# A convolution-attention layer with a sorted mixture of experts on one core: row outputs on another engine, shares and counts a step later, first halves apart, two pairs in both directions

## The chip, the cores and the metric

The kernel runs on one core of a Trainium2 chip. The metric is the device time in microseconds (us) of one execution. Of the engines, TensorE (PE) multiplies matrices, VectorE (DVE), ScalarE (ACT) and GpSimd (POOL) work on elements, and SyncE (SP) issues most of the transfers between the core's memory and DRAM. Each engine takes its own list of instructions, and semaphores hold them back until what they need is there.

## The reference

The input x has 4 batches of 32 channels, 128 x 128, all float32. Each batch becomes a matrix q of 128 rows (32 channels times 2 x 2 pixel places) by 4096 columns. Note the axis: the rows of the similarity matrix are q's *columns* as the kernel lays them out, 4096 of them in groups of 128.

```python
xs = x.reshape(B, C, h, R, w, R).transpose(0, 1, 3, 5, 2, 4).reshape(B, C * R * R, h, w)
energy = jnp.einsum('bci,bcj->bij', q, q)              # (4096, 4096), symmetric
d = jnp.sqrt(jnp.diagonal(energy, axis1=1, axis2=2))
attn = jax.nn.softmax(energy / (d[:, :, None] * d[:, None, :]), axis=-1)
out = gamma * jnp.einsum('bcj,bij->bci', q, attn).reshape(...) + xs
...
t = t + _L1_attn_ref(_ln_t(t), Wk, Wq, Wv)             # linear attention, 8 heads
t = t + _L1_ffn_ref(_ln_t(t), router_w, router_b, expert_w, expert_b)   # 2 of 8 experts for each token
```

The first layer is a softmax attention without separate queries and keys, so the matrix before the division by the row sums is symmetric. The second layer treats the result as 4096 tokens of 128 numbers per batch: layer norm, a linear attention over the whole batch, layer norm, a router, and for each token a weighted sum of two expert products.

## The kernel before

**Attention.** The 4096 columns of a batch are eight chunks of 512. `attend` walks rows i = 0 to 7, and in row i the chunks jc = i (the diagonal) and 0 to i - 1. One step is one group of 128 rows of chunk jc against the 512 columns of chunk i: a product `pe` (L497), its exponential `pr` with the sums over columns (L500, ScalarE), and two steps later the product `po` (L404) that adds to the row's output. Since the matrix is symmetric, a pair (i, jc) is exponentiated once. What chunk jc gets from it needs the transposed block: VectorE transposes 32 x 32 blocks of pr into F (L356), `move` writes F to DRAM as `blocks`, `bring` reads it back as G in another order (L455), and `transposed_share` multiplies it (`pg`, L362), takes its sums on ScalarE (`junk`, L367) and adds the result to the earlier chunk's output `o` (L372, VectorE). A share is four sub-steps, at most one for each step, and each needs the one PSUM bank `pg`; the row output needs the one bank `po`. When a row's last product is done the bank is copied out as `o` (L409), and only then can the next row's first `po` begin.

For the last row of the last batch, pairs with jc of 4 or more do not go by DRAM: G is made by 16 direct transfers. The very last pair (7, 6) has no F at all; it is computed in both directions, that is, with four more products `pe_back`, four more exponentials and four products `back` (L462 on).

**Time in the program.** TensorE, VectorE, ScalarE and SyncE run in the program's own order (`manual_schedule`), so the order in which the Python code issues is the order in each queue; GpSimd has its own. The code keeps a `clock` in units of a 128 x 128 product: a step adds 8, a share's sub-step 4, so a full step has 12. A share is due when the clock has passed `LAG` since its G was asked for. Other work is cut into generators, and each `yield` ends a piece:

```python
timed.append((setup_sorting(), 58, 70, 9))     # (pieces, begin %, end %, count) of a batch's attention
...
if clock[0] >= stream[1]:
    stream[1] = clock[0] + PACE                # PACE = 10: a piece of layer 1 about every step
```

Every call of a stream advances it by two yields. From 84% of a batch's attention on, its `layer1` joins the stream and runs under the next batch's attention; only the last batch's has nothing to run under and ends in `last_parts`.

**prep** loads a quarter of a batch (two chunks, L275, four transfers on SP's queue), transposes it (`ptq`, L306; `qT`, L295), takes squares and sums (L317, L318), the power -1/2 on GpSimd (L166, `rn`), scales (`qs`, L327) and transposes back (`ptn`, L335) into the two normalised chunks `qn` (L333). For the first quarter of the first batch all of it stands ahead of the first step.

**layer1.** `close_rows(kc)` finishes a quarter, once both of its chunks have all their shares: sums and reciprocals (`den`, `rd`, `rdx`, L613 to L618), their transposes (`pbd`, L640), the division (`df`, L627), the residual (L647), statistics (L650, L563 to L571), normalised rows (L577, on VectorE L660) and the Gram matrix (`pgram`, L602), with the transposes `ptx` (L582) of the last batch. In batches 0 to 2 the tokens are sorted by expert: `sorted_experts` adds up one-hot rows (`runs`, L843 to L846, VectorE), counts them by a product (`pcnt`, L853), works out places (to L887), scatters rows to DRAM `xs` with GpSimd's indirect transfers (L902), loads tiles of one expert, multiplies (`pys`, L958), stores `ys`, and gathers them (L1020) into the sum (L992). `setup_sorting` makes constants and fills xs eight times 624 KB from x on ScalarE's queue (L156), so that unused rows hold numbers.

Of the kernel before, what the change touches and what calls it, by code (L numbers as in the profile page):

```python
# [12 lines left out]
F32 = mybir.dt.float32  # L13
BF16 = mybir.dt.bfloat16
U32 = mybir.dt.uint32
AF = mybir.ActivationFunctionType
ALU = mybir.AluOpType
# [5 lines left out]
def kernel(  # L23
# [44 lines left out]
    nc = tc.nc  # L68
    P = 128
    B, C, H, W = x.shape  # L70
    N = (H // 2) * (W // 2)
    NB = N // P
    CH = 512
    NCH = N // CH
    NJ = CH // P
# [12 lines left out]
    ppool = ctx.enter_context(tc.tile_pool(name="ppool", bufs=6))  # L88
# [11 lines left out]
    def psum_t(name):  # L100
        return ps_t.tile([P, CH], F32, tag="pt", name=name)
# [63 lines left out]
    def pow_neg_half(dst, src):  # L165
        pinned(nc.gpsimd.tensor_tensor(dst, src, neg_half.to_broadcast(list(src.shape)), ALU.pow))  # L166
# [100 lines left out]
    def tokens(ap, b):  # L267
        return ap[b].rearrange("c (s k r) w -> s r c k w", s=2, r=2)

    def load_tokens(dst, b, k0, nk):  # L270
        src = tokens(x, b)
        for s in range(2):
            for r1 in range(2):
                p0 = s * 64 + r1 * 32
                nc.sync.dma_start(dst[p0 : p0 + 32], src[s, r1, :, k0 : k0 + nk, :])  # L275


    def prep(b, kc, st):

        if b == 0:  # L280
            if kc == 0:
                st["all"] = big1.tile([P, 4, 8, HW2, 2], F32, tag="T", name="xx_0")
            xx = st["all"][:, kc]
        else:
            xx = xin.tile([P, 8, HW2, 2], F32, tag="xx", name=f"xx_{b}_{kc}")
        load_tokens(xx.rearrange("p k w r -> p k (w r)"), b, 8 * kc, 8)
        qT = qpool.tile([P, 2, NJ, P], F32, tag="qT", name=f"qT_{b}_{kc}")
        st.setdefault("qT", {})[2 * kc] = qT[:, 0]
        st["qT"][2 * kc + 1] = qT[:, 1]
        yield  # L290
        yield
        yield from idle(1)

        def load_half(g, pt):
            nc.vector.tensor_copy(  # L295
                qT[:, :, 2 * g : 2 * g + 2, :].rearrange("p s j (r c) -> p (j r) s c", c=64),
                pt.rearrange("p (m s c) -> p m s c", s=2, c=64),
            )

        for g in range(2):  # L300
            yield
            pt, done = hold(f"ptq_{b}_{kc}_{g}", partial(load_half, g))
            for jj in range(2):
                for r2 in range(2):
                    k = 4 * g + 2 * jj
                    nc.tensor.transpose(  # L306
                        pt[:, ts(2 * jj + r2, P)], xx[:, k : k + 2, :, r2].rearrange("p k w -> p (k w)"), ident
                    )
            yield
            done()  # L310
        yield
        yield
        ss = stat.tile([P, 2 * NJ], F32, tag="ss", name=f"ss_{b}_{kc}")
        rn = stat.tile([P, 2 * NJ, 1], F32, tag="rn", name=f"rn_{b}_{kc}")
        for s in range(2):
            sq = work.tile([P, NJ, P], F32, tag="qs", name=f"sq_{b}_{kc}_{s}", bufs=2)
            nc.vector.tensor_tensor(sq, qT[:, s], qT[:, s], ALU.mult)  # L317
            nc.vector.tensor_reduce(ss[:, ts(s, NJ)], sq, AX.X, ALU.add)  # L318
            if s == 1:
                pow_neg_half(rn[:, :, 0], ss)  # L320
            yield
            yield
        yield from idle(1)
        scaled = []
        for s in range(2):
            qs = work.tile([P, NJ, P], F32, tag="qs", name=f"qs_{b}_{kc}_{s}", bufs=2)
            nc.vector.tensor_tensor(qs, qT[:, s], rn[:, ts(s, NJ)].to_broadcast([P, NJ, P]), ALU.mult)  # L327
            scaled.append(qs)
        for s, qs in enumerate(scaled):
            yield  # L330
            qn = npool.tile([P, CH], F32, tag="qn", name=f"qn_{b}_{2 * kc + s}")
            st.setdefault("qn", {})[2 * kc + s] = qn
            pt, done = hold(f"ptn_{b}_{kc}_{s}", lambda p, qn=qn: nc.scalar.activation(qn, p, AF.Copy))  # L333
            for j in range(NJ):
                nc.tensor.transpose(pt[:, ts(j, P)], qs[:, j, :], ident)  # L335
            yield
            done()
        yield
        yield
# [2 lines left out]
    tick = [0]  # L342
    queued = []
    late = []
    LAG = 45
    exps = []

    def after(ticks, f):
        queued.append((tick[0] + ticks, f))
# [32 lines left out]
    def attend(b, st):  # L382
# [11 lines left out]
        for i in range(NCH):  # L394
            ending = b == B - 1 and i == NCH - 1
            order = list(range(i - 1)) + [i, i - 1] if ending else [i] + list(range(i))
            row = {"left": NJ * (i + 1) + NJ - 1}

            def values(w, blk, lo, hi, i=i, row=row):
                start = "po" not in row  # L400
                if start:
                    row["po"] = ps_o.tile([P, CH], F32, tag="po", name=f"po_{b}_{i}")
                row["left"] -= 1
                nc.tensor.matmul(  # L404
                    row["po"][:, lo:hi], qT[blk // NJ][:, blk % NJ, :], w, start=start, stop=(row["left"] == 0)
                )
                if row["left"] == 0:
                    o = opool.tile([P, CH], F32, tag="o", name=f"o_{b}_{i}")
                    nc.vector.tensor_copy(o, row["po"])  # L409
                    st["o"].append(o)  # L410

            def below(tiles, blks, i=i, values=values):
# [19 lines left out]
                done()  # L432

            def move(F, i, jc):
                last = b == B - 1 and i == NCH - 1 and jc >= NCH - 4
                if last:
                    G = gpool.tile([P, 4, NJ, P], F32, tag="G", name=f"G_{b}_{i}_{jc}")
                    for a in range(4):
                        for q in range(4):
                            nc.sync.dma_start(  # L440
                                G[ts(q, S), a].rearrange("p ib f -> p (ib f)"),
                                F[ts(a, S), q].rearrange("p ib j c -> p (ib j c)"),
                            )
                    late.append((clock[0] + 58, transposed_share(b, st, i, jc, G)))
                    return
                blocks = dram.tile([4, S, 4, CH], F32, tag="blocks", name=f"blocks_{b}_{i}_{jc}", bufs=4)
                nc.sync.dma_start(
                    blocks.rearrange("a p q f -> (a p) q f"), F.rearrange("p q ib j c -> p q (ib j c)")
                )
                after(3, partial(bring, blocks, i, jc))  # L450
# [6 lines left out]
                    )  # L457
                late.append((clock[0] + LAG, transposed_share(b, st, i, jc, G)))

            def back(w, j, i=i):  # L460

                if j == 0:  # L462
                    while len(held) > 1:
                        held[0]()
                    banks[0] = 2
                    row["back"] = psum_t(f"back_{b}")
                nc.tensor.matmul(row["back"], qT[i][:, j, :], w, start=(j == 0), stop=(j == NJ - 1))
                if j == NJ - 1:
                    nc.vector.tensor_tensor(st["o"][i - 1], st["o"][i - 1], row["back"], ALU.add)
                    st["got"][i - 1] += 1  # L470
                    banks[0] = 3

            for jc in order:
                both = ending and jc == i - 1
                for j in range(NJ if both else 0):
                    yield
                    tick[0] += 1
                    pe = ps_e.tile([P, CH], F32, tag="pe", name=f"pe_{b}_back_{j}")
                    nc.tensor.matmul(pe, qn[i][:, ts(j, P)], qn[jc], start=True, stop=True)
                    pr = ppool.tile([P, CH], F32, tag="pr", name=f"pr_{b}_back_{j}")  # L480
                    nc.scalar.activation(pr, pe, AF.Exp, accum_out=sums[:, NJ * i + j, jc : jc + 1])
                    after(2, partial(back, pr, j))
                    turn_tick()
                    clock[0] += 2 * NJ
                    step_share()
                    yield
# [48 lines left out]
    def layer1(b, st):  # L535
# [290 lines left out]
        def sorted_experts(h):  # L826
# [18 lines left out]
            while shift < HR:  # L845
                nc.vector.tensor_tensor(dst[:, pad:], src[:, pad:], src[:, pad - shift : pad - shift + HR], ALU.add)  # L846
                src, dst = dst, src
                shift *= 2
            yield
            run = src[:, pad:]  # L850
            counts, places = small("count", [P, 2, E]), small("at", [P, HR, 1])
            pc, done = hold(f"pcnt_{b}_{h}", lambda p: nc.vector.tensor_copy(counts.rearrange("p n e -> p (n e)"), p[:, : 2 * E]))
# [343 lines left out]
    first = prep(0, 0, states[0])  # L1196
    next(first)
    load_weights()
    for _ in first:
        pass  # L1200

    ordered = ExitStack()
    ordered.enter_context(tc.manual_schedule(engines=ENGINES))
    timed = []
    for b in range(B):

        if b == 0:
            for kc, begin, end in ((1, 0, 5), (2, 6, 20), (3, 25, 45)):
                timed.append((prep(0, kc, states[0]), begin, end, 12))
            timed.append((setup_weights(), 46, 58, 9))  # L1210
            timed.append((setup_sorting(), 58, 70, 9))
        if b + 1 < B:
            nxt = states[b + 1]
            timed.append((prep(b + 1, 0, nxt), 66, 82, 12))
# [72 lines left out]
```

## Time and profile before

| | us |
|---|---|
| median of 3 runs | 1778.02 |
| lowest and highest | 1777.36, 1779.36 |
| profiled execution | 1780.28 |
| its span, first to last instruction | 1778.5 |
| TensorE busy | 1672.9 (94%) |
| VectorE, ScalarE busy | 899.4, 912.0 (51% each) |
| GpSimd busy | 514.6 (29%) |
| DMA, mean over the span | 187 GB/s |

In the profile PE is TensorE's matmuls and PEld its weight loads. A float32 product is two instructions and so stands as x2. Time in brackets is what the engine sat idle just before, with the instruction that ended the wait. Busy time of TensorE runs past its real end, since matmuls are pipelined: the distance between starts is the true price. Times within a run count from the first instruction.

### The profile page before, as it was taken

What the parts mean: (1) busy time and instruction counts of PE and PEld (TensorE: products, weight loads), DVE (VectorE), ACT (ScalarE), POOL (GpSimd) and SP (SyncE); (2) the same over time, 40 slices, a digit from 0 to 9 for tenths busy, and PEclk for the clock granted to TensorE, in tenths of its full rate; (3) what the DMA queues carried; (4) which work ended last, traced back from release to release, by engine and by line L of the source; (5) the groups of instructions that cost most, each with busy time, mean ns of one, the idle gap of its engine ahead of it and who ended that gap; (6) DMA issues with size and microseconds to landing.
All of it is one profiled execution on the core that took longest, in us unless ns stands there. A gap on an engine that the chain in (4) does not pass through costs nothing.

```text
span 1778.5 us, 20656 instructions
## 1 busy us (share of the span) xinstructions
PE 1672.9 (94%) x5572; PEld 890.8 (50%) x5572; DVE 899.4 (51%) x2249; ACT 912.0 (51%) x2843; POOL 514.6 (29%) x553
## 2 busy tenths in 40 slices
PE   7999999999999999989999999999999999889787
PEld 4544544455554555445554455545555455434533
DVE  3333333456475335565468334556647533455587
ACT  3455444464565544445565554546456554445366
POOL 1000000011017604550014631661101760670156
PEclk9999999999999999999999999999999999999799
DMA  2666788854557989884357789996445699995001
GB/s 59 166 178 166 214 235 249 222 130 121 152 150 220 265 235 266 240 263 120 122 163 215 231 242 260 262 255 187 136 151 149 214 271 250 269 281 132 1 13 36
DMA packets 218563, 332.91 MB, mean 187 GB/s; under 512 B 24528, under 2 KB 136656, under 8 KB 204368
## 3 DMA queue, kind: packets, MB, share of 16 engines
q1 hardware_dynamic: 202192, 299.18, 60.2%
q0 software_dynamic: 12288, 25.19, 4.8%
q10 hardware_dynamic: 3968, 7.22, 1.3%
q8 instruction: 46, 0.75, 0.2%
q14 instruction: 69, 0.57, 0.1%
HBM read 172.50 MB, written 162.00 MB: 188 GB/s over the span
## 4 chain that ended last, share of the span: by engine, by line
PE 66%; DMA 15%; DVE 13%; issue 2%; SPq 2%; ACT 2%; POOL 1%; DVEq 0%; ACTq 0%; POOLq 0%
PE po L404 20%; PE pe L497 17%; PE pg L362 15%; DMA ys<-xn 4%; DMA blocks<-F 4%; PE py L1099 2%; DMA G<-blocks 2%; DVE F L356 2%; PE pgram L602 2%; PE pys L958 2%; DMA yb<-ys,place 2%; PE pat L714 1%; DMA xx<-in_x_dram 1%; DVE df L627 1%; PE ptd L430 1%
## 5 line engine op out<-in xcount | busy, mean ns | idle before, releaser
L500 ACT ACTIVATE pr<-pe 128x512 f32<-128x512 f32 (+1 forms) x576 | 322.9, 561 | 592.4 <-PE pe L497 572.9
L404 PE MATMUL po<-pr,qT 128*128 128x512 f32 (+3 forms) x1152 | 555.3, 564 | 13.4 <-DVE o L409 13.0
L362 PE MATMUL pg<-G,qT 128*128 128x512 f32 x888 | 457.9, 597 | 28.3 <-DVE o L372 21.8
L497 PE MATMUL pe<-qn,qn 128*128 128x512 f32 x896 | 460.7, 596 | 0.7 <-ACT pr L500 0.6
L356 DVE STREAM_TRANSPOSE F<-pr 128x512 f32<-128x512 f32 x444 | 311.5, 704 | 199.8 <-ACT pr L500 198.5
L404 PEld LDWEIGHTS po<-pr,qT 128*128 128x128 f32 x1152 | 216.6, 192 | 258.8 <-issue 230.2
L367 ACT ACTIVATE junk<-G 128x512 bf16<-128x512 f32 x444 | 275.4, 620 | 6.8 <-issue 4.6
L362 PEld LDWEIGHTS pg<-G,qT 128*128 128x128 f32 x888 | 163.4, 191 | 216.1 <-issue 157.4
L1020 POOL DMA_INDIRECT yb<-ys,place x192 | 186.5, 971 | 265.9 <-ACT pr L500 138.5
L902 POOL DMA_INDIRECT xs<-xn,place x192 | 186.1, 969 | 110.8 <-ACT pr L500 53.0
L497 PEld LDWEIGHTS pe<-qn,qn 128*128 128x128 f32 x896 | 155.7, 192 | 118.9 <-issue 111.8
L372 DVE TENSOR_TENSOR o<-o,pg 128x512 f32<-128x512 f32 x111 | 75.4, 679 | 212.0 <-PE pg L362 211.8
L940 DVE COPY xn<-pys 128x256 f32<-128x256 f32 (+1 forms) x120 | 49.2, 416 | 216.4 <-DMA ys<-xn 120.0
L166 POOL TENSOR_TENSOR rn<-ss,neg_half 128x8 f32<-128x8 f32 x16 | 29.5, 1841 | 377.1 <-DVE ss L318 377.0
L500 ACT ACTIVATION_READ_ACCUMULATOR pr<-pe 128x1 f32 x576 | 111.9, 194 | 0.0
L935 ACT ACTIVATE xn<-pys 128x256 f32<-128x256 f32 (+1 forms) x120 | 44.9, 378 | 122.5 <-PE pys L965 122.5
L166 POOL TENSOR_TENSOR rsf<-dm_f,neg_half 128x8 f32<-128x8 f32 (+1 forms) x15 | 26.2, 1744 | 259.1 <-DVE sv_f L569 259.1
L958 PEld LDWEIGHTS pys<-ew_sb,xn 128*128 128x128 f32 x468 | 69.0, 191 | 56.6 <-issue 44.6
L992 DVE SCALAR_TENSOR_TENSOR acc<-yb,weight,acc 128x128 f32<-128x128 f32 x192 | 64.1, 339 | 62.7 <-DMA yb<-ys,place 42.8
L497 PE MATMUL pe<-qn 128*128 128x512 f32 (+3 forms) x256 | 92.2, 444 | 0.0
L166 POOL TENSOR_TENSOR rsa<-dm_a,neg_half 128x8 f32<-128x8 f32 x16 | 26.3, 1641 | 217.3 <-DVE sv_a L569 217.3
L367 ACT ACTIVATION_READ_ACCUMULATOR junk<-G 128x1 f32 x444 | 85.0, 191 | 0.0
(178 smaller groups left out, 1549.0 us busy)
## 6 DMA issues: line engine op xcount, KB each, us to landing
blocks<-F SPq DMA_DIRECT2D x109, 1024.0 KB
G<-blocks SPq DMA_DIRECT2D x436, 256.0 KB
xn<-xs SPq DMA_DIRECT2D x114, 128.0 KB
ys<-xn SPq DMA_DIRECT2D x114, 128.0 KB
xx<-in_x_dram SPq DMA_DIRECT2D x64, 128.0 KB
T<-in_x_dram SPq DMA_DIRECT2D x64, 128.0 KB
out_dram<-acc SPq DMA_DIRECT2D x128, 64.0 KB
t<-T SPq DMA_DIRECT2D x12, 512.0 KB
```

Source lines behind the costliest of these rows:

```text
L166: pinned(nc.gpsimd.tensor_tensor(dst, src, neg_half.to_broadcast(list(src.shape)), ALU.pow))
L356: f()
L362: nc.tensor.matmul(pg.rearrange("p (a f) -> p a f", a=4), st["qT"][i][:, ib, :], G[:, :, ib], start=(ib == 0), stop=(ib == NJ - 1),)
L367: nc.scalar.activation(junk, G[:, :, ib], AF.Copy, accum_out=st["sums"][:, NJ * i + ib, jc : jc + 1])
L372: nc.vector.tensor_tensor(o, o, pg.rearrange("p (a j c) -> p a j c", a=4, c=S), ALU.add)
L404: nc.tensor.matmul(row["po"][:, lo:hi], qT[blk // NJ][:, blk % NJ, :], w, start=start, stop=(row["left"] == 0))
L497: nc.tensor.matmul(pe[:, c0:], qn[jc][:, ts(j, P)], qn[i][:, c0:], start=True, stop=True)
L500: nc.scalar.activation(pr[:, c0:], pe[:, c0:], AF.Exp, accum_out=sums[:, t, i : i + 1]).ins
L902: inst = nc.gpsimd.indirect_dma_start(xs[h], offset(place[:, i, k : k + 1]), xn[:, k, :], None)
L958: nc.tensor.matmul(p[:, 2 * P + j * D : 2 * P + j * D + D], bufs[4 + g % 2][:, j, :], weights[:, bass.ds(begins[2 * (g % 2) + j], D)], sta ...
L992: nc.vector.scalar_tensor_tensor(a[:, k % 4, :], yb[k // 4][:, i, k % 4, :], weight[:, i, k, :], a[:, k % 4, :], ALU.mult, ALU.add)
L1020: inst = nc.gpsimd.indirect_dma_start(yb[k // 4][:, i, k % 4, :], None, ys, offset(place[:, i, k : k + 1]))
```

## The change

Row outputs are copied out of PSUM by ScalarE. `LAG` is 57 instead of 45. `sorted_experts` has two more yields between the runs and the count. The first quarter's loads are split over two queues, its powers are taken for each half by itself, and what is left of it after the first chunk's `qn` joins the timed work of the first batch. The last row of the last batch takes both of its last pairs, (7, 5) and (7, 6), in both directions, and the direct transfers serve pairs 3 and 4. `setup_sorting` is spread up to 98% of the first batch.

```diff
-    def load_tokens(dst, b, k0, nk):
+    def load_tokens(dst, b, k0, nk, queues=(nc.sync, nc.sync)):
...
-                nc.sync.dma_start(dst[p0 : p0 + 32], src[s, r1, :, k0 : k0 + nk, :])
+                queues[r1].dma_start(dst[p0 : p0 + 32], src[s, r1, :, k0 : k0 + nk, :])
...
-        load_tokens(xx.rearrange("p k w r -> p k (w r)"), b, 8 * kc, 8)
+        first = b == 0 and kc == 0
+        load_tokens(
+            xx.rearrange("p k w r -> p k (w r)"), b, 8 * kc, 8, (nc.sync, nc.scalar if first else nc.sync)
+        )
...
-            if s == 1:
+            if first:
+                pow_neg_half(rn[:, ts(s, NJ), 0], ss[:, ts(s, NJ)])
+            elif s == 1:
                 pow_neg_half(rn[:, :, 0], ss)
...
-    LAG = 45
+    LAG = 57
...
+            twice = (i - 2, i - 1) if ending else ()
...
-                    nc.vector.tensor_copy(o, row["po"])
+                    nc.scalar.activation(o, row["po"], AF.Copy)
...
-                last = b == B - 1 and i == NCH - 1 and jc >= NCH - 4
+                last = b == B - 1 and i == NCH - 1 and jc >= NCH - 5
...
-            def back(w, j, i=i):
+            def back(w, j, jc, i=i):
...
-                    nc.vector.tensor_tensor(st["o"][i - 1], st["o"][i - 1], row["back"], ALU.add)
-                    st["got"][i - 1] += 1
+                    nc.vector.tensor_tensor(st["o"][jc], st["o"][jc], row["back"], ALU.add)
+                    st["got"][jc] += 1
...
-                both = ending and jc == i - 1
+                both = jc in twice
...
-                    after(2, partial(back, pr, j))
+                    after(2, partial(back, pr, j, jc))
...
                 shift *= 2
+            yield
+            yield
             yield
             run = src[:, pad:]
...
-    for _ in first:
-        pass
+    while 0 not in states[0].get("qn", {}):
+        next(first)
+    next(first)
...
-    timed = []
+    timed = [(first, 0, 1, 4)]
...
-            timed.append((setup_sorting(), 58, 70, 9))
+            timed.append((setup_sorting(), 58, 98, 9))
```

More of the change, by code (lines that the diff above doesn't have):

```diff
@@ L465, in back @@
                     banks[0] = 2
-                    row["back"] = psum_t(f"back_{b}")
+                    row["back"] = psum_t(f"back_{b}_{jc}")
                 nc.tensor.matmul(row["back"], qT[i][:, j, :], w, start=(j == 0), stop=(j == NJ - 1))
                 if j == NJ - 1:
-                    nc.vector.tensor_tensor(st["o"][i - 1], st["o"][i - 1], row["back"], ALU.add)
-                    st["got"][i - 1] += 1
+                    nc.vector.tensor_tensor(st["o"][jc], st["o"][jc], row["back"], ALU.add)
+                    st["got"][jc] += 1
                     banks[0] = 3
             for jc in order:
-                both = ending and jc == i - 1
+                both = jc in twice
                 for j in range(NJ if both else 0):
@@ L477, in attend @@
                     tick[0] += 1
-                    pe = ps_e.tile([P, CH], F32, tag="pe", name=f"pe_{b}_back_{j}")
+                    pe = ps_e.tile([P, CH], F32, tag="pe", name=f"pe_{b}_back_{jc}_{j}")
                     nc.tensor.matmul(pe, qn[i][:, ts(j, P)], qn[jc], start=True, stop=True)
-                    pr = ppool.tile([P, CH], F32, tag="pr", name=f"pr_{b}_back_{j}")
+                    pr = ppool.tile([P, CH], F32, tag="pr", name=f"pr_{b}_back_{jc}_{j}")
                     nc.scalar.activation(pr, pe, AF.Exp, accum_out=sums[:, NJ * i + j, jc : jc + 1])
-                    after(2, partial(back, pr, j))
+                    after(2, partial(back, pr, j, jc))
                     turn_tick()
```

## The prediction

> **What bounds the kernel now.** I read the page first, then the table of waits, then the timelines of TensorE, VectorE and ScalarE at the longest waits, and last the chain that ended last. The page's own rows say that TensorE sets the time: it is busy 94% of the span, and its slices are nines but for a few places.
>
> ```profile
> PE   7999999999999999989999999999999999889787
> ...
> L404 PE MATMUL po<-pr,qT 128*128 128x512 f32 (+3 forms) x1152 | 555.3, 564 | 13.4 <-DVE o L409 13.0
> ```
>
> A product of 512 columns stands as x2 and 1.02 us, but the next starts 0.86 us after it; so 0.43 us is the price of one of the two, and 128 columns cost 0.11. Taking these prices from every start-to-start distance leaves 145.8 us of the span in which TensorE did not advance at full speed. Only that can be won. Who ends these pauses:
>
> ```profile
> PE pg L362 <- DVE o L372: 21.8, 15, 3.6
> PE po L404 <- DVE o L409: 13.0, 9, 3.6
> ...
> PE pcnt L853 <- DVE runs L846: 6.2, 3, 2.1
> ```
>
> Columns are total us, times, longest. The last two are touched by the change. Their longest cases in TensorE's timeline:
>
> ```profile
> 410.61 0.59 PE L497 MATMUL pe<-qn 128*128 128x256 f32 x2
> 414.79 2.08 PE L404 MATMUL po<-pr,qT 128*128 128x512 f32 x2 [3.58 <-DVE o L409]
> ...
> 519.39 1.02 PE L362 MATMUL pg<-G,qT 128*128 128x512 f32 x2
> 522.48 0.39 PE L853 MATMUL pcnt<-runs,rank_below 128*128 128x8 f32 x2 [2.06 <-DVE runs L846]
> ```
>
> and what VectorE and then ScalarE did at the first of them:
>
> ```profile
> 413.52 0.61 DVE L618 TENSOR_SCALAR rdx<-rd,gam 128x256 f32<-128x256 f32 x2
> 414.05 0.68 DVE L409 COPY o<-po 128x512 f32<-128x512 f32 x1
> ```
>
> ```profile
> 417.33 0.28 ACT L500 ACTIVATE pr<-pe 128x128 f32<-128x128 f32 x1 [5.61 <-PE pe L497]
> ```
>
> The row's sum was complete at about 410.8, yet VectorE copied it at 414.05, behind a whole closing block (den, rdx and the statistics before them). ScalarE meanwhile had nothing from 411.7 to 417.3. In the last two rows of TensorE the count is asked for while VectorE still adds up the runs.
>
> The third place is a transfer that comes late, in the table by stretch and in the chain of waits:
>
> ```profile
> 240.00:290.00 50.00, 43.99 (x104) 19.30 (x103) 16.31 (x24) 19.85 (x60) 0.00 (x0) 0.97 0.91 269
> ```
>
> ```profile
> 245.84 5.48 DMA xs<-in_x_dram
> 251.38 6.10 DMA blocks<-F
> ...
> 259.17 4.51 DMA G<-blocks
> 263.68 3.48 issue
> ```
>
> The last three numbers of the stretch are clock, DMA share and GB/s: the eight fills of xs, 624 KB each, have the DMA engines 91% busy, and a block on its way to DRAM and back waits behind them. The fourth place is the end of attention, in the chain:
>
> ```profile
> 1662.40 0.62 DVE rdx L618 x2
> ...
> 1675.09 2.08 PE pgram L602 x8
> ```
>
> In the same chain the last product takes 0.86 from 1655.28, to 1656.14; the last quarter's rdx is made only at 1662.4, since VectorE first closes the quarter before.
>
> **What the Trainium skill says.** "PSUM — Partial Sum Buffer", section "Engine vs sequencer instructions": ScalarE and VectorE take their queues strictly in order. The trace agrees: the copy at 414.05 stood behind rdx for 3.3 us with its input ready. "TensorE: Matmul & The Clock Gate", part 1, on the clock gate: after idling the array runs at half rate until a free-running window of activity has passed. The trace agrees: the product after the 414.79 stall has 2.08 us in place of 1.02. So a stall costs more than its idle time. "DMA: Bandwidth & Descriptors", "Issuing engines are not separate DMA queues": a second issuer saves only issue time. The trace of before cannot tell; it has one issuer at the start.
>
> **The change part by part.** The sum is made against the profiled execution, 1780.3 us (span 1778.5), which is 2.3 above the median; the same 2.3 is taken off at the end.
>
> *Row outputs on ScalarE.* 32 copies leave VectorE (0.69 each) and 32 of 0.60 come to ScalarE, the duration of its qn copy of the same form; the skill's price for such a copy (page "VectorE: DVE Perf Modes", the errata section) gives an estimate of 0.66 against 0.57, the same order. Only the place in the queue matters. Loss by the pitch, over the 9 to 10 us around each of the three long stalls (414.8, 837.1, 1257.5): 5.5, 5.4, 5.4, half-rate products included. Nine more waits, at 27, 42, 67, 549, 705, 971, 1126, 1392 and 1456, have 0.4 to 1.0 each, 5.3 together. On ScalarE the copy is behind one exponential and ahead of the next, and done some 0.9 us after the sum. The long stalls go; what is late next is rdx: without the stall pbd would be asked for near 413.5, and VectorE has rdx at 414. I leave 0.9 each for that: 16.3 - 2.7 = 13.6. Of the small ones, the rows that have no share to stand between keep theirs: 5.3 - 1.5 = 3.8. Behind the copy on ScalarE stand the share's sum over G (0.62 + 0.19) and the next exponential; products two steps later wait for that one, and a step has 2.58 us of TensorE against some 2.1 of ScalarE with the copy, so nothing. Sum 17.4 (bounds 12 and 20).
>
> *Shares a step later.* LAG + 12 is one step. No instruction and no DMA is added; a share's four products and its o add (L372) move by a step. G has 2.6 us more to arrive, its buffer is free 2.6 later, with four steps to spare before the third block after it is brought. It puts a share of 0.86 between a row's last product and the next row's first, which is part of what I counted above; alone 0 (bounds -5 and +3, since an o add may fall before or behind a closing block).
>
> *Counts a step later.* The three stalls cost 4.5, 2.8 and 4.5 with their half-rate products: 11.7. VectorE has the runs at 522.4; TensorE would ask at 519.39 + 0.86 + 2.58 = 522.8. They go by 0.4 us, so I take 10.5 (bounds 6 and 11.7). Everything behind moves too: 32 scatters of 0.97 on GpSimd per half, the loads and stores on SP's queue, the gathers, by a step per half, 5 us at a batch's end. The last batch that sorts ends its gathers at 1602 and the kernel ends at 1778: hidden. The next batch's closing needs its sort done, which is so at 1554, and begins at 1611.
>
> *Fills of xs over 58 to 98% instead of 58 to 70.* Eight issues on ScalarE's queue, 0.50 each, now some 18 us apart instead of 5. TensorE lost 8.5 us between 262 and 285. From 285 to 405 the DMA share is 0.83 and then 0.46, so there is room. 7 (bounds 3 and 8.5).
>
> *First rows' halves.* Two of four loads go to ScalarE's queue, ahead of its three small ones and the table load; its first work comes at 15.7, so these are hidden. An issue takes 0.60 (eight in 4.79), so the last is issued 1.2 earlier, and SP's next four too; the bytes cannot come faster, I take 0.8. The power is split: one more GpSimd instruction of 1.67, which delays the second half only. The first half no longer waits for the second's reduction (0.6): 0.8 + 0.6 = 1.4. Against it, four transposes and one copy enter the first row, where TensorE waits for ScalarE anyway: 0. I take 1.4 (bounds 0 and 2.2).
>
> *Last two pairs in both directions.* For pair 5 of the last row go four transposes of VectorE (0.70), four shares (0.86 on TensorE, 0.81 on ScalarE) and one G; in come four pe and four back products (0.86 each) and four exponentials. Net +3.4 on TensorE; VectorE gains 2.8; SP has 5 DMAs fewer, since pair 3 takes over the 16 direct ones. Gain: chunks 4 and 5 are complete nine steps before the end, by the order of steps, instead of two. Their closing (pbd 0.4, two gram groups 1.8) and the quarter before's two transposes (0.9) go under attention, where TensorE has no gap: 3.4 + 3.1 = 6.5 later. Then the end: from the last product to the copied gram 23.6 us (1656.14 to 1679.77). After: 1.0 for the copy, 2.8 df, 1.2 T, 1.7 statistics, 1.0 their close, 1.9 GpSimd, 0.6 to the first gram, 3.8 for gram without the transposes between: 14.0. Gain 9.6 - 6.5 = 3 (bounds -1 and 6).
>
> *Not shown by any row:* what VectorE, no longer stalled with TensorE, makes late next. Loss of 2 taken (bounds -3 and 8, the largest being a wait of half a us in two steps of each batch's closings).
>
> Sum: 17.4 + 10.5 + 7 + 1.4 + 3 - 2 = 37.3. 1780.3 - 37.3 - 2.3 = 1740.7.
>
> **The rivals.** *The DMA-bound stages take it back.* From 640 to 800, 1060 to 1230 and 1430 to 1625 the DMA engines are 93 to 94% busy, and TensorE loses 46 us there, mostly at pg behind an o add that waits behind a gathered row. Sorting a step later and shares a step later set these anew. For it: a time set by transfers does not shrink with TensorE's. Against: the transfers are the same. A third more, 15 us: 1756. *The waits only change their names* (the change does not do what it says): the long row stalls become waits for rdx and pg, the runs are still not ready. Then 13.6 and 10.5 are missing: 1765. Against: ScalarE's empty stretch above. *Slower:* the copy is in ScalarE's queue before the row's last product has ended and holds the next exponential, so that TensorE runs out of pr. It decides from 0.62 us a row (the other gains, 19.9, over 32 rows); at 1.0 a row the time is 1778 + 32 - 19.9 = 1790. Against: at 410.8 the next product's exponential could start only at 411.2 anyway.
>
> **How the numbers follow.** Forecast 0.75, alone 1731 to 1751; the DMA stages 0.13; names only 0.07; slower 0.05. The range 1730 to 1760 takes in the first two. About 0.2%, 3.6 us, is what a measurement of this kernel can tell from no change: faster 0.93, same 0.02, slower 0.05.
>
> **What would show it.** po waits on o for under 3 us in all, none over 1; no wait of pcnt over 0.3; no pause of 3 us between 245 and 405; the first pe near 15; the last quarter's rdx within 2 us of the last product. Wrong if ScalarE's exponentials at row starts lie later than TensorE can bear, if the loss in the three DMA stages grows by over 10 us, or if rdx or pg takes over stalls of 3 us at 413, 836 and 1256.

## The result, and the profile after

The changed kernel takes 1750.95 us, median of 4 runs (1748.38 to 1754.33), against 1778.28 us for the kernel before in the same comparison: a ratio of 0.9847, interval [0.9825, 0.9869]. That is 27.3 us less; the forecast, 1740.7, would have been 37.6 less. The profiled execution took 1748.38 us, its span is 1746.6.

The page of the changed kernel, TensorE's slices and the row of the products that the rows' sums are made of:

```profile
PE   7999999999999999989999999999999999989777
...
L410 PE MATMUL po<-pr,qT 128*128 128x512 f32 (+3 forms) x1152 | 550.4, 560 | 0.5 <-ACT o L415 0.5
```

The slices hardly differ (near the end one 8 has become a 9 and, in the tail, another a 7): tenths of 44 us are too coarse for this change. But the idle time in front of these products fell from 13.4 us to 0.5. The table of waits of the changed kernel (total us, times, longest):

```profile
DVE acc L1000 <- DMA yb<-ys,place: 40.1, 31, 3.8
PE pg L367 <- DVE o L377: 25.3, 13, 6.2
DVE acc L1000 <- DMA acc<-t: 22.1, 4, 6.3
...
PE pys L966 <- DVE xn L948: 8.3, 3, 4.0
...
PE pbd L646 <- DVE rdx L624: 1.8, 1, 1.8
...
PE po L410 <- ACT o L415: 0.5, 2, 0.3
```

The row of po is the smallest of those shown, and TensorE has no row any more in which pcnt waits for the runs. But pg, which the change was not aimed at, waits longer than before (its longest rose from 3.6 us to 6.2), and VectorE's wait for the load of acc has risen to 22.1 us; in the kernel before it was 10.2:

```profile
DVE acc L992 <- DMA acc<-t: 10.2, 3, 4.6
```

So something was gained and something was given back. To see how much of each and where, I took TensorE's loss in the prediction's way (start-to-start distances, less 0.43 us per 512 columns) and cut it by stage. "Sort" reaches from a batch's first scatter to 5 us after its last gather is issued, "counts" is the 20 us before each first scatter, "rows" is all else up to the last product (from 25 to 200 us, from 200 us to the first counts, the first rows of batches 1 and 2, and what is left of attention). Every number is of the profiled execution, in us:

| kernel | to 25 us | rows | counts | sort, batches 0, 1, 2 | last product to gram | after it | sum |
|---|---|---|---|---|---|---|---|
| before | 9.4 | 40.6 | 13.0 | 15.3, 15.3, 13.8 | 18.2 | 20.2 | 145.8 |
| changed | 8.8 | 10.2 | 5.1 | 22.3, 17.9, 17.4 | 10.7 | 19.1 | 111.5 |
| difference | -0.6 | -30.4 | -7.9 | +13.2 | -7.5 | -1.1 | -34.3 |

TensorE's own work is 1622.0 us in place of 1618.6, 3.4 more for the second pair, as forecast; -34.3 + 3.4 = -30.9, and the two spans differ by 31.9; the first product also starts 0.94 earlier (5.80 in place of 6.74), which this sum does not count. **The aimed-at stalls went; the stages that sort and gather took 13 us back.**

How it looks where the gain is. In the stretch from 240 to 290 us of the changed kernel, the table by stretch (same columns as before):

```profile
240.00:290.00 50.00, 50.00 (x134) 23.74 (x133) 18.29 (x27) 25.74 (x84) 1.63 (x1) 1.00 0.84 234
```

TensorE is busy for all of 50 us (43.99 before) and the DMA share is 0.84 in place of 0.91. At the first row of the next batch, where TensorE stood for 3.58 us, ScalarE's timeline and then TensorE's:

```profile
399.21 0.60 ACT L415 ACTIVATE o<-po 128x512 f32<-128x512 f32 x1 [0.28 <-PE po L410]
```

```profile
400.30 1.02 PE L410 MATMUL po<-pr,qT 128*128 128x512 f32 x2
...
405.71 0.60 PE L646 MATMUL pbd<-ident,rdx 128*128 128x128 f32 x4
```

The copy follows the row's sum at once; the next row's first product at 400.30 and pbd at 405.71 have no bracket, so neither waits: the wait for rdx that I feared in its place did not come.

How it looks where the loss is: TensorE of the changed kernel at the first closing of batch 1, while batch 0 gathers.

```profile
764.97 1.02 PE L410 MATMUL po<-pr,qT 128*128 128x512 f32 x2
772.23 2.08 PE L367 MATMUL pg<-G,qT 128*128 128x512 f32 x2 [6.24 <-DVE o L377]
774.10 1.92 PE L503 MATMUL pe<-qn,qn 128*128 128x512 f32 x2
775.80 1.91 PE L410 MATMUL po<-pr,qT 128*128 128x512 f32 x2
777.51 1.42 PE L367 MATMUL pg<-G,qT 128*128 128x512 f32 x2
```

VectorE and SyncE's queue in the same place:

```profile
764.00 0.74 DVE L1000 SCALAR_TENSOR_TENSOR acc<-yb,weight,acc 128x128 f32<-128x128 f32 x2 [5.97 <-DMA acc<-t]
764.65 2.78 DVE L633 TENSOR_TENSOR df<-o,pbd 64x512 f32<-64x512 f32 x4
...
768.72 1.22 DVE L653 TENSOR_TENSOR T<-T,df 128x1024 f32<-128x1024 f32 x1
769.97 0.87 DVE L656 BATCH_NORM_STATS2 bs_a<-T 128x6 f32<-128x128 f32 x4
...
771.49 0.69 DVE L377 TENSOR_TENSOR o<-o,pg 128x512 f32<-128x512 f32 x1
```

```profile
753.08 1.75 SPq L461 DMA_DIRECT2D G<-blocks  x4
754.92 1.86 SPq L1010 DMA_DIRECT2D out_dram<-acc  x4
756.99 0.34 SPq L1026 DMA_DIRECT2D acc<-t  x1
```

Read it backwards. TensorE waits for the o add (L377, 771.49). That add stands behind a whole closing block (df, T, statistics) in VectorE's queue, and the block stands behind one gathered row's sum that waits 5.97 us for acc, which was asked for at 756.99, right behind four stores, which in turn stand behind a read of G. What "PSUM — Partial Sum Buffer", section "Engine vs sequencer instructions", says in the Trainium skill, that VectorE takes its queue strictly in order, is what makes a 6 us wait for one row of a sum into a 6 us wait of TensorE: nothing of the closing block needed acc. After it the products take up to 2.08 us in place of 1.02, and start up to 1.87 us apart in place of 0.86; this agrees with what "TensorE: Matmul & The Clock Gate", part 1, on the clock gate, says of an array that has idled.

### The profile page after: what moved, and what is told of

The parts are those of the page before. It is cut to its first block, busy times and chain, and to the rows that moved or that the text cites. A ratio compares the mean times of both kernels' runs of the same rounds, so it can differ in the third digit from the quotient of the medians.

```text
span 1746.6 us, 20682 instructions
## 1 busy us (share of the span) xinstructions
PE 1666.0 (95%) x5580; PEld 891.6 (51%) x5580; DVE 878.6 (50%) x2213; ACT 929.6 (53%) x2875; POOL 509.2 (29%) x554
## 5 line engine op out<-in xcount | busy, mean ns | idle before, releaser
L503 PE MATMUL pe<-qn,qn 128*128 128x512 f32 x896 | 463.9, 600 | 1.8 <-ACT pr L506 1.8
L503 PEld LDWEIGHTS pe<-qn,qn 128*128 128x128 f32 x896 | 155.7, 192 | 117.4 <-issue 107.9
L377 DVE TENSOR_TENSOR o<-o,pg 128x512 f32<-128x512 f32 x110 | 75.1, 682 | 235.0 <-PE pg L367 234.7
L166 POOL TENSOR_TENSOR rn<-ss,neg_half 128x8 f32<-128x8 f32 (+1 forms) x17 | 26.8, 1578 | 459.7 <-DVE ss L321 401.4
L503 PE MATMUL pe<-qn 128*128 128x512 f32 (+3 forms) x256 | 91.4, 439 | 0.7 <-ACT qn L338 0.7
```

The costliest lines, as they stand in the source:

```text
L377: nc.vector.tensor_tensor(o, o, pg.rearrange("p (a j c) -> p a j c", a=4, c=S), ALU.add)
L503: nc.tensor.matmul(pe[:, c0:], qn[jc][:, ts(j, P)], qn[i][:, c0:], start=True, stop=True)
```

## The experiments

Three comparisons of four kernels. The first ran on another chip, on which the kernel before takes 1833.5 us and the changed kernel was not run, so those four are set against each other and against the kernel before; the second and the third, each on a chip of its own, have the changed kernel among them. Times are medians, losses are of the one profiled execution of each kernel. The kernel before was profiled only beside the first result. The sort stages of the changed kernel lost 57.6, 65.5 and 60.7 us in its three profiles, so a difference of a few us between two kernels tells nothing there.

### Four parts undone, one at a time

**u_rows**, the copies on VectorE again:

```diff
-                    nc.scalar.activation(o, row["po"], AF.Copy)
+                    nc.vector.tensor_copy(o, row["po"])
```

> The changed kernel (1751 us) with the row outputs copied by VectorE again, all else kept. Theory A (the parts add, by the places where they act): the waits of po on o come back, long ones at the first row of batches 1 to 3, softened or not by the share that now stands there; 13 to 20 us slower, 1764 to 1771. Rival B (the later share alone had filled those pauses): within 4 us of the changed kernel, and at most 3 us of waits of po on o.

**u_lag**, the shares at their old time:

```diff
-    LAG = 57
+    LAG = 45
```

> The changed kernel with LAG at 45 again, all else kept. Theory A (the later share only covers the short row pauses, since ScalarE took the long ones): 2 to 5 us slower, 1753 to 1756, the loss in the three transfer-bound stages unchanged near 51 us. Rival B (the later share is what gave back 5 to 7 us in those stages): 3 to 7 us faster, 1744 to 1748, and that loss back near 46.

**u_counts**, the counts at their old time:

```diff
                 shift *= 2
-            yield
-            yield
             yield
```

> The changed kernel without the two added yields ahead of the count. Theory A (the later count saves its three stalls, partly given back in a wait of pg on an o add some 1.5 us long in each batch): 6 to 8 us slower, 1757 to 1759, stalls of pcnt of 2 us back and those of pg at the second count gone. Rival B (the step later is also what set the long pauses in the transfer-bound stages, 6.2 and 4.5 us at pg and 4.0 at pys): these vanish too, and the time is within 2 us of the changed kernel.

**u_xs**, the fills of xs close together again:

```diff
-            timed.append((setup_sorting(), 58, 98, 9))
+            timed.append((setup_sorting(), 58, 70, 9))
```

> The changed kernel with the eight fills of xs pressed into 58 to 70% again. Theory A (G and the next quarter come late behind the fills): 6 to 9 us slower, 1757 to 1760, with 6 to 9 us of TensorE's loss between 240 and 290. Rival B (a share that is due a step later waits 2.6 us longer for G, so the later share had removed the worst of it already): 2 to 5 us slower, 1753 to 1756, and no single pause over 2 us at pg there.

Measured, with TensorE's loss in three of the stages and the part of "rows" from 200 us to the first counts, us:

| kernel | time | ratio to before | rows | of it 200 to counts | counts | sort |
|---|---|---|---|---|---|---|
| u_rows | 1812.99 | 0.9879 [0.985, 0.9909] | 17.3 | 6.7 | 5.1 | 114.6 |
| u_lag | 1800.53 | 0.9819 [0.9795, 0.9844] | 16.0 | 6.8 | 5.7 | 100.0 |
| u_counts | 1788.51 | 0.9752 [0.9723, 0.9781] | 10.2 | 4.4 | 7.2 | 91.7 |
| u_xs | 1812.0 | 0.9859 [0.9826, 0.9892] | 18.0 | 12.1 | 5.1 | 110.1 |

The stages outside the sort can be read. Putting the fills back brings 12.1 - 4.4 = 7.7 us of loss, in the two places where it was before; TensorE's timeline of u_xs:

```profile
267.51 1.10 PE L367 MATMUL pg<-G,qT 128*128 128x512 f32 x2 [3.49 <-DMA G<-blocks]
275.73 0.99 PE L309 MATMUL ptq<-ident,xx 128*128 128x128 f32 x4 [1.98 <-DMA xx<-in_x_dram]
```

So the fills are worth what was forecast (7), and the later shares don't cover for them. Putting the copies back costs only 17.3 - 10.2 = 7.1 us at the rows, far less than the 17.4 of the forecast. And the version without the later counts is the fastest of the four: its counts stay cheap (7.2, not 13.0), since LAG 57 alone takes most of those stalls.

Of what was expected, theory A of u_xs holds where it acts (7.7 us, with a pause of 3.49 at pg). u_rows lies between its two theories: 7.1 us at the rows, where po waits for its copy 7.9 us in all but never over 2.2. In u_counts the 2 us waits of pcnt did not come back (none is over 0.7). The times that were expected beside the changed kernel can't be compared on this chip. The sort stages of this chip lose twice what they lose elsewhere; that is told of in the last section, and no verdict is built on it.

### The gain alone, and the two small parts

**after_again** is the changed kernel once more.

> The changed kernel itself, as the measure for the others of this group, since the first group ran where the kernel before takes 1833 us. Theory C (there the whole machine answers later by the same share): ratio to before 0.985 as at first. Rival D (the later signals of that place fall on the transfer-bound stages, which the later steps made tighter): 0.977 to 0.982 or, if they hit the changed kernel harder, over 0.988; without the added yields the ratio was 0.975 there.

**rows_xs** is the kernel before with two edits of the change alone:

```diff
-                    nc.vector.tensor_copy(o, row["po"])
+                    nc.scalar.activation(o, row["po"], AF.Copy)
...
-            timed.append((setup_sorting(), 58, 70, 9))
+            timed.append((setup_sorting(), 58, 98, 9))
```

> The kernel before with two parts alone: row outputs copied by ScalarE, fills of xs spread to 98%. Theory A (parts add by place: 20 us of row pauses and 8.5 us beside the fills): 27 us faster than before where that takes 1778, ratio 0.984 to 0.987, so these two alone bring what the whole change brings. Rival E (without the later share the row pauses only shrink, and the freed time is lost again in the transfer-bound stages): 10 to 18 us faster, ratio 0.990 to 0.994.

**u_pairs**, only the last pair in both directions:

```diff
-            twice = (i - 2, i - 1) if ending else ()
+            twice = (i - 1,) if ending else ()
...
-                last = b == B - 1 and i == NCH - 1 and jc >= NCH - 5
+                last = b == B - 1 and i == NCH - 1 and jc >= NCH - 4
```

> The changed kernel with only its very last pair in both directions, and the direct transfers for pairs 4 and 5, as before. Theory A (9.6 us less at the end against 6.5 us more work under attention): 2 to 4 us slower than the changed kernel of this group, with the last quarter's rdx some 6 us after the last product again. Rival F (the end is bound by the last quarter's own chain and the work moved costs as much as it saves): within 1.5 us.

**u_first**, the first rows prepared at one go from one queue:

```diff
-        first = b == 0 and kc == 0
+        first = False
...
-    while 0 not in states[0].get("qn", {}):
-        next(first)
-    next(first)
+    for _ in first:
+        pass
...
-    timed = [(first, 0, 1, 4)]
+    timed = []
```

> The changed kernel with the first quarter prepared in one piece and loaded by SyncE alone, as before. Theory A: 1.4 to 1.8 us slower than the changed kernel of this group, the first pe at 16.3 in place of 14.2. Rival G (the half that is left comes into the first row at half clock and takes back what the earlier start gives): the first row's output is copied within 0.5 us of the same moment, and the time is the same.

Measured, the kernel before at 1784.37 here:

| kernel | time | ratio to before | rows | counts | sort | last product to gram |
|---|---|---|---|---|---|---|
| after_again | 1754.38 | 0.9833 [0.9817, 0.9849] | 10.3 | 5.1 | 65.5 | 11.1 |
| rows_xs | 1760.63 | 0.9876 [0.9855, 0.9897] | 20.0 | 12.2 | 44.3 | 17.3 |
| u_pairs | 1759.81 | 0.9857 [0.9835, 0.9879] | 12.0 | 5.1 | 62.8 | 17.0 |
| u_first | 1751.89 | 0.9823 [0.9807, 0.9839] | 10.2 | 5.1 | 59.7 | 11.1 |

Two edits of six bring 23.7 of the 30.0 us, and they leave the sort stages where they were in the kernel before (44.3 against 44.4, the latter from the profile beside the first result). So neither the copies nor the fills are what raised the loss there. The remaining edits take 9.7 more at the rows, 7.1 at the counts and 6.2 at the end, and are worth only 6.3 us together, because the sort stages lose more. The 21 us by which the two profiles differ there are too many, though: the profiled execution of after_again is the slowest of its five (1759.19) and that of rows_xs the fastest of its five (1755.87). If all of that scatter lies in the sort stages, some 12 are left at the medians (an estimate from these distances: 4.8 and 4.8).

rows_xs brings a little less than its theory A had (27 us, ratio up to 0.987).

Without the second pair the time is 5.4 us more, where theory A had 2 to 4 (the intervals overlap a little); by the stages the end loses 17.0 - 11.1 = 5.9 more, less the 3.4 of work saved. TensorE's timeline of u_pairs has the place:

```profile
1640.16 0.60 PE L588 MATMUL ptx<-ident,xn 128*128 128x128 f32 x4
1653.76 6.07 PE L608 MATMUL pgram<-xn 128*128 128x128 f32 x32 [12.99 <-ACT xn L583]
```

With it, in the changed kernel, the same stretch is split and shorter:

```profile
1635.90 0.60 PE L646 MATMUL pbd<-ident,rdx 128*128 128x128 f32 x4
1645.74 3.45 PE L608 MATMUL pgram<-xn 128*128 128x128 f32 x16 [8.28 <-ACT xn L583]
1649.57 2.10 PE L703 MATMUL pgv<-wvx,gram 128*128 128x408 f32 x6 [0.38 <-DVE gram L687]
```

The first rows' halves show no gain: u_first is 2.5 us below its control, with intervals that overlap, and its loss up to 25 us is 9.5 against 9.7. Its first pe starts at 15.57 instead of 13.96, but the first row's output is copied at 25.95 against 25.75, and in the other two profiles of the changed kernel at 25.09 and 26.58. That is rival G.

### The two later steps, together, alone and neither

What is left are the two edits that set work a step later. The four corners of that square: **after_third** (both, the changed kernel), **u_counts_again** (shares later, the edit of u_counts), **u_lag_again** (counts later, the edit of u_lag) and **no_steps** (both of these edits, so neither is later).

> The changed kernel itself, the measure for the three others, which leave out the later count, the later share, and both. Theory H (steps that were moved later make the transfer-bound sort stages lose more): ratio 0.983 to 0.986, and TensorE's loss over the three sort stages 55 to 66 us, where the kernel before and the kernel with two parts alone had 44.

> The changed kernel without the two yields ahead of the count. Theory H: the sort stages lose 42 to 50 us instead of 55 to 66, the stretch around each count 2.4 instead of 1.7, and the time is 8 to 15 us under the changed kernel of this group. Rival A (parts add: the later count saves its stalls): 2 to 8 us over it.

> The changed kernel with LAG at 45. Theory H: the sort stages lose 5 to 10 us less, the first rows of batches 1 to 3 lose some 5 more in all; between 6 us under and 1 us over the changed kernel of this group. Rival B (the later share alone is at fault in the sort stages): 8 to 15 us under it.

> The changed kernel with neither the later count nor the later share. Theory H with effects that add: the sort stages lose 42 to 46 us as before the change, the counts 3.7 each again; 6 to 12 us under the changed kernel of this group, level with the one that leaves out only the count. Rival J (each of the two spoils the order only beside the other): more than 3 us away from what the two single differences add up to.

Measured, the kernel before at 1782.56:

| kernel | LAG | counts | time | ratio to before | rows | counts | sort |
|---|---|---|---|---|---|---|---|
| after_third | 57 | later | 1754.03 | 0.9837 [0.9814, 0.9859] | 10.2 | 5.1 | 60.7 |
| u_counts_again | 57 | as before | **1740.45** | 0.9765 [0.9737, 0.9793] | 10.3 | 7.2 | 46.0 |
| u_lag_again | 45 | later | 1744.88 | 0.9799 [0.9775, 0.9824] | 17.7 | 5.7 | 43.2 |
| no_steps | 45 | as before | 1759.28 | 0.9854 [0.9828, 0.988] | 20.2 | 14.3 | 50.7 |

If the effects of the two edits added up, leaving out both would change the time by the sum of leaving out each: -13.6 and -9.2, so -22.8. It is +5.2. **Each of the two helps while the other is absent, and together they undo most of it.** Theory H gave u_counts_again rightly (8 to 15 us under) and u_lag_again wrongly (at most 6 under; rival B had 8 to 15); for no_steps rival J holds. At the counts they are two ways to the same gain: 14.3 with neither, 7.2 and 5.7 with one, 5.1 with both, so the second of them has 2.1 or 0.6 us left to win. In the sort stages both together cost 60.7 against 46.0 and 43.2.

The waits of u_counts_again beside those of the changed kernel above, with the same row of acc at L998:

```profile
PE pg L367 <- DVE o L377: 17.8, 11, 4.9
...
DVE acc L998 <- DMA acc<-t: 6.9, 2, 3.8
...
PE pcnt L859 <- DVE runs L852: 3.1, 6, 0.7
```

acc costs VectorE 6.9 us in place of 22.1 (22.8 in after_third), and pcnt is back with no wait over 0.7. This goes through all ten profiles that are not of the first comparison's chip: the five with both steps have 18.0 to 23.4 us of this wait for acc, the five others, the kernel before among them, 6.9 to 10.3. The row of pg is 17.8 here and 28.0 in after_third; these 10.2 are the larger part of the 14.7 between their sort stages. Its VectorE and its SyncE queue at the place that was shown above:

```profile
758.62 0.70 DVE L998 SCALAR_TENSOR_TENSOR acc<-yb,weight,acc 128x128 f32<-128x128 f32 x2
...
761.07 2.81 DVE L633 TENSOR_TENSOR df<-o,pbd 64x512 f32<-64x512 f32 x4 [0.51 <-PE pbd L646]
...
768.72 0.69 DVE L377 TENSOR_TENSOR o<-o,pg 128x512 f32<-128x512 f32 x1
```

```profile
744.71 1.74 SPq L461 DMA_DIRECT2D G<-blocks  x4
746.54 0.38 SPq L453 DMA_DIRECT2D blocks<-F  x1
747.02 3.27 SPq L1008 DMA_DIRECT2D out_dram<-acc  x4
750.34 0.58 SPq L1024 DMA_DIRECT2D acc<-t  x1
```

A batch has eight loads of acc, each for four groups of 128 tokens, and the one that the changed kernel asks for at 756.99 is the seventh. Here the seventh is asked for at 750.34, 6.7 us earlier, so that the sum that needs it, at 758.62, does not wait. The sum still stands ahead of df; what has gone is its wait. The closing block starts as soon as pbd is there, and TensorE pauses for 1.57 us at 769.46 where it paused for 6.24.

Why the load is late is seen in SyncE's queue. In both kernels it stands behind four stores of acc, and these behind a read of G, which SyncE issues only when the block it reads has been written (a wait of up to 9.0 us in the changed kernel). The sums that the stores carry off end at about the same time, 743.58 in the changed kernel and 743.84 here. But there the stores stand behind the read at 753.08 and go out 11.3 us after the sums, here behind that at 744.71 and 3.2 us after them. Batch 1 repeats it: its seventh load is asked for at 1174.54 in the changed kernel, and its sum waits 3.92 us; here at 1162.40, and it does not wait. In after_third the sum that waited at 764.00 has its wait in front again, so this is no accident of one execution:

```profile
764.11 0.74 DVE L1000 SCALAR_TENSOR_TENSOR acc<-yb,weight,acc 128x128 f32<-128x128 f32 x2 [5.33 <-DMA acc<-t]
764.76 2.78 DVE L633 TENSOR_TENSOR df<-o,pbd 64x512 f32<-64x512 f32 x4
```

u_counts_again is the best version found: 13.6 us below the changed kernel beside it and 42 below the kernel before. It is the change less two lines.

## Why the prediction was right in its direction, and where its sum failed

- **Bound and direction.** TensorE's pauses were all that could be won, and 34.3 of 145.8 us went. The time lies in the range; it lies at the upper end of the forecast's own case, since a loss that I had as a rival joined it. That the sum missed by only 10 us is luck in part: the rows and fills brought 30.4 us in the profile, where the forecast had 17.4 + 7 = 24.4, and this hid some of what the sort stages took back.
- **Row outputs, 17.4.** The stalls went as told: po waits 0.5 us in all, and rdx did not take over. But the term is not the copies' alone. Taking out 7.7 for the fills, the rows lost 32.9 us before, 20.2 with the copies alone (no_steps), 17.3 with LAG 57 in their place (u_rows, on the other chip) and 10.2 with both. So the copies bring 12.7 by themselves and about 7 beside LAG 57.
- **Shares a step later, 0.** This term was mis-sized. Beside the copies, and without the later counts, it takes the rows from 20.2 to 10.3 and the counts from 14.3 to 7.2; the time falls by 18.8 us, from no_steps to u_counts_again. I had written that a share between two rows "is part of what I counted above" and gave it nothing of its own. A product of 0.86 that needs neither the row's copy nor the runs covers their wait wherever it comes between.
- **Counts a step later, 10.5.** The stalls went (13.0 to 5.1), and alone, beside the old LAG, the step is worth 14.4 (no_steps to u_lag_again). But LAG 57 alone brings the counts to 7.2, from 13.0 in the kernel before or 14.3 in no_steps. Beside LAG 57 it saves 2.1 at the counts and costs 14.7 in the sort stages (after_third against u_counts_again). This is the step that failed: "Everything behind moves too ... hidden". I looked at whether the sort is done in time and not at when its loads are asked for and what its sums stand ahead of in VectorE's queue on the way. The two terms were also added as if each had stalls of its own, though they share most of those at the counts. There is also a new pause at 529.95, of 1.39 us, where a pg waits for its o add just ahead of a count.
- **Fills of xs, 7.** 7.7 when put back; the stretch from 240 to 290 is full.
- **First rows' halves, 1.4.** The first pe starts at 14.19 in place of 16.35, earlier than the forecast's 15; but with the old start it is at 15.57 in u_first and 15.60 in rows_xs, so about 1.4 of the 2.2 is the edit's, which is the term itself. No gain is seen at the end: the first row's output comes at the same moment with and without it.
- **Last two pairs, 3.** Work +3.4 as forecast. From the last product's end (1633.2) to the copied gram 16.0 us, forecast 14.0, before 23.6. The comparison gives 5.4 and the stages 2.5 (5.9 - 3.4), both within the bounds.
- **What no row shows, -2 (to -8).** This is where a loss such as that of the sort stages should have been. It came to 13 in the first profile, 21 and 16 in the next two. By the forecast's own three stretches it was 46 before and 53, 59 and 56 in these profiles, so its sign of being wrong, 10 us more, was reached in two of three. The rival "the DMA-bound stages take it back" had 15 us and a chance of 0.13. Its size was right, and it named the place, pg behind an o add that waits behind a gathered row; its reason, a time set by transfers, holds only in part. Over the gathers of batches 0 and 1 the DMA engines have a share of 0.91 and 0.91 in the changed kernel and of 0.93 and 0.94 in u_counts_again, and from the first gather to the last sum it takes 113 and 111 us in the one and 112 and 111 in the other. So the gathers go at the same pace in both. What differs is when the loads of acc are asked for and what VectorE has queued behind the wait for them.
- **The other rivals** are out: names did not merely change, and a pe waited for an exponential's release for 1.8 us in all (the page's row of L503).

What stays open: how the two steps together put the stores, and with them the load of acc, behind a later read of G. The traces show where the load stands in each kernel and what waits behind it; that its place costs the sort stages what they lose is argued from this, since no kernel was run with only this load moved. In batch 2 the changed kernel has a pause of 4.12 us at pg (at 1559.15) behind waiting sums as well, which was not followed further. no_steps loses 50.7 us in the sort stages where rows_xs loses 44.3, although they differ only in the first rows and the last pairs; but the profiled execution of no_steps is the slowest of its five, that of rows_xs the fastest of its five, so this may be scatter.

## What to carry to other kernels

When two streams of work are merged into one in-order queue, a step's delay on one of them changes what each wait stands ahead of: cost a moved step by finding which of its instructions wait for a transfer, what the issue of that transfer stands behind, and what is queued right behind the wait, and test delays together and apart. Two edits that fill the same bubble are not to be added up; take the one with the larger gain and then look what is left for the other. A part of a change whose own stall is gone without it is the first thing to leave out.

## What the runs showed of the hardware that was not expected

On the chip of the first comparison the kernel before takes 1833.5 us, 3% more than in the other three comparisons (1778 to 1784), at the same program. The traces of its four kernels hold 12 to 16 waits each that none of the ten traces from the other chips has: ScalarE or VectorE stands, and the trace names no instruction of the core as releaser. In the case shown here the input had been computed long before. ScalarE's timeline of u_rows, and TensorE's:

```profile
1419.10 0.60 ACT L506 ACTIVATE pr<-pe 128x512 f32<-128x512 f32 x1 [0.79 <-PE pe L503]
...
1430.68 0.60 ACT L506 ACTIVATE pr<-pe 128x512 f32<-128x512 f32 x1 [10.29 <-remote]
```

```profile
1421.05 1.02 PE L503 MATMUL pe<-qn,qn 128*128 128x512 f32 x2
...
1431.42 2.08 PE L503 MATMUL pe<-qn,qn 128*128 128x512 f32 x2 [5.06 <-ACT pr L506]
```

The second exponential is that of the product at 1421.05, which ended at 1422.07, 8.6 us before. Such waits add up to 69 us on ScalarE in u_rows and to 33 to 46 in the other three of that comparison. All of them lie during, or within 1.3 us of, GpSimd's indirect transfers, which it issues one every 1.26 us here and at the same pace on the other chips. Whether these hold up the signal, and why on one chip and not on the others, stays open.
